# Edge rows in fewer packets, a reordered first group and a wo low part on another engine, in a graph attention layer

## The chip, the cores and the metric

The kernel runs on one core of one Trainium2 chip. The time is the device time in microseconds. A profiled execution gives a span, from its first to its last instruction, beside its own time.

## The reference

The layer normalizes 384 node vectors of 1024 numbers, applies ReLU, and runs 16-head attention over them with two projections in a row for each of query, key and value. The edges (6528 pairs of source and destination, each with a type) make an additive mask; pairs without an edge get minus infinity.

```python
h = jnp.maximum(_layernorm(x, axis=-1), 0.0)
q = h @ wq.T + bq;  k = h @ wk.T + bk;  v = h @ wv.T + bv
q2 = (q @ wiq.T + biq).reshape(N, H, D).transpose(1, 0, 2)     # N = 384, H = 16, D = 64
k2 = (k @ wik.T + bik).reshape(N, H, D).transpose(1, 0, 2)
v2 = (v @ wiv.T + biv).reshape(N, H, D).transpose(1, 0, 2)
mask = jnp.full((N, N), -jnp.inf).at[src, dst].set(w[edge_type - 1])   # the diagonal is always set
attn = softmax(einsum('hnd,hmd->hnm', q2, k2) / 8 + mask)
x + (attn @ v2, heads joined) @ wo.T + bo
```

## The kernel before

**Numbers in two parts.** Every matrix product is made of three fp32r products: high part by high part, high by low, and low by high. An operand is split by rounding it to fp32r (the high part) and subtracting that from the original (the low part). For the weights this is `split_hi` (L77, a copy on ScalarE, or L75 on VectorE) and `split_lo` (L82, a subtraction on VectorE unless another engine is given). `mm3` issues the three products (L367 high by high, L368 with the weight's low part in the projections, L369 with the activations' low part). In the output projection the roles are exchanged, and the weights stream.

**Weights in chunks.** There are 56 weight chunks of 128 x 1024 numbers, in the order v, q, iv, k, then iq and ik in turn, then eight of wo. `load(w)` (L65) brings a chunk into one of three `raw` buffers through SP's queue; a chunk's load can only start when the chunk three before it has been split. All loads named here are issued by SP, in program order.

**The order of the work.** The order is written out by hand: each engine runs its instructions in the order in which the program issues them.

**The start.** SP issues the first block of x (128 tokens, 512 KB), then the edge rows `er`, the two other blocks of x (all L96; the edge rows are L98), weight chunk 0, the edge columns `ed`, chunk 1 and two small tables. GpSimd turns the edge rows into one key per edge in `key_rows` (L182 to L184: integer to float, source times 384, plus destination), and SP writes the keys to a table `krow` in DRAM (L185), from which the row loads (L205) read them back for all partitions. Then chunk 2 is loaded. For each block t of 128 tokens, VectorE takes the statistics (L251, L254), ScalarE negates the mean (L257) and subtracts it from the first half of the columns (L280); GpSimd does the second half of blocks 0 and 1 (L282), VectorE both halves of block 2 (L284). TensorE transposes the two halves (L292), ScalarE takes the ReLU as high part (`ln_hi`, L298), and VectorE later the low part (`ln_lo`, L303). `hT` then holds the activations, tokens along the columns: 0 to 127 from block 0, 128 to 255 from block 1, 256 to 383 from block 2. On ScalarE the two `ln_hi` of block 0 stand ahead of the L257 and L280 of block 1.

GpSimd also splits weight chunk 0, in halves: high part L344, low part L346. Chunk 1 gets its high part on ScalarE (L77), after all six `ln_hi`, and its low part on GpSimd (L82), after chunk 0 and a conversion of the edge columns (L150).

**The first group.** The first output chunk (w == 0) is made of 24 products of 128 x 128 by 128 x 384, all on L414: the eight high-by-high ones first, then four at a time the ones with the low part of the weight and of the activations. The second group follows with L367, L368, L369 for each of eight k.

**The attention and the output projection.** Attention runs over 48 steps (16 heads by 3 blocks) with projection work filled in between. In step i TensorE makes the scores of step i (`do_S`, L694, one of two `s` banks), VectorE reduces those of step i - 1 (`do_ttr`, L700, which frees the bank), ScalarE takes the exponential, GpSimd normalizes (L709, after VectorE's reciprocal L708), and TensorE transposes (L714). From step 37 on, `wo_prep` splits the wo chunks 2 to 7 in the steps of `WSTEPS`. Its tuple `OPOOL` lists the chunks whose low part GpSimd makes. Chunks 4 to 6 go to a part of the buffer that held q.

```python
    def wo_prep(k):
        ...
        split(WO + k, nc.gpsimd if k in OPOOL else None, dst, k in ODVE)
        load(WO + k + 2)
```

The first half of the output projection's sums (chunks 0 to 3) is added to the residual by VectorE (`ysum`, L654) from step 43 on; chunk 4 is first used after that, in the second half.

Of the kernel before, what the change touches and what calls it, by code (L numbers as in the profile page):

```python
# [10 lines left out]
I32 = mybir.dt.int32  # L11
AF = mybir.ActivationFunctionType
OP = mybir.AluOpType

N, D, NT, KT, NP = 384, 1024, 3, 8, 8
E = 6528
EC = E // 128
# [5 lines left out]
def gnn_kernel(ctx: ExitStack, tc: tile.TileContext, x, edges, erows, etw, wq, wk, wv, wiq, wik, wiv, wo,  # L23
# [6 lines left out]
    nc = tc.nc  # L30
# [13 lines left out]
    def bank(tag):  # L44
        return psum.tile([128, 512], F32, tag=tag, name=tag, bufs={"g": 3, "a": 1}.get(tag, 2))
# [11 lines left out]
    raw, whl = {}, {}  # L57
# [33 lines left out]
    xt = [xall[:, t * D:(t + 1) * D] for t in range(NT)]  # L91
    xn = [xall[:, (NT + t) * D:(NT + t + 1) * D] for t in range(NT)]
    ert = work.tile([128, N], F32, tag="e", name="er", bufs=EB)
    er = ert[:, :2 * EC].bitcast(I32)
    for t in range(NT):
        nc.sync.dma_start(xt[t], x[t * 128:(t + 1) * 128, :])  # L96
        if t == 0:
# [28 lines left out]
    krow = dram.tile([EC, 128], F32, name="krow")  # L126
# [48 lines left out]
            nc.gpsimd.tensor_tensor(val, val, t, OP.add)  # L175

    krt = work.tile([128, N], F32, tag="e", name="kr", bufs=EB)
    kf = ert[:, :2 * EC]

    def key_rows():  # L180

        nc.gpsimd.tensor_copy(kf, er)  # L182
        nc.gpsimd.tensor_scalar(kf[:, :EC], kf[:, :EC], float(N), None, op0=OP.mult)
        nc.gpsimd.tensor_tensor(krt[:, :EC], kf[:, :EC], kf[:, EC:], OP.add)  # L184
        nc.sync.dma_start(krow.rearrange("c j -> (c j)").rearrange("(p e) -> p e", p=128), krt[:, :EC])  # L185

    rows = {}
    PA = 6
# [81 lines left out]
    def ln_row():  # L270

        ps = bank("t")
        for t in range(NT):
            nc.tensor.transpose(ps[:, t * 128:(t + 1) * 128], rstd[:, t:t + 1].to_broadcast([128, 128]), ident)
        nc.scalar.activation(rrow, ps[:, :N], AF.Copy)
# [35 lines left out]
    mask_consts()  # L311
    warm(WARM[0])
    key_rows()
    load(2)
    for s in range(NTAB):
# [55 lines left out]
    def colmm(ps, w, src, k):  # L371
        hi, lo = whl[w]
        mm3(ps[:, :N], hi[:, k * 128:(k + 1) * 128], lo[:, k * 128:(k + 1) * 128],
            src[:, 0, k, :], src[:, 1, k, :], k == 0, k == KT - 1)
# [5 lines left out]
    def evac_row(ps, hi, lo, bias):  # L380
        f = work.tile([128, N], F32, tag="e", name="f", bufs=EB)
        nc.vector.tensor_tensor(f, ps[:, :N], rrow, OP.mult)  # L382
        nc.scalar.activation(hi, f, AF.Identity, bias=bias)  # L383
        post.append(lambda: nc.vector.scalar_tensor_tensor(lo, f, bias, hi.bitcast(F32), op0=OP.add, op1=OP.subtract))
# [4 lines left out]
    def flush(last=False):  # L389
        while pend:  # L390
            pend.pop(0)()
        while last and post:
            post.pop(0)()

    def slot_head(w):
        if w > 0:
            split_hi(w + 2)
        if w != 1:
            flush()
        split_lo(w + 2)  # L400
        while post:
            post.pop(0)()
        load(w + 4)

    def proj(src, dst, bidx, extra=None):
        nonlocal w
        for m in range(8):
            slot_head(w)
            ps = bank("g")
            if w == 0:  # L410
                for a, b, ks in ((0, 0, range(KT)), (1, 0, range(4)), (0, 1, range(4)), (1, 0, range(4, KT)),
                                 (0, 1, range(4, KT))):
                    for k in ks:
                        nc.tensor.matmul(ps[:, :N], whl[0][a][:, k * 128:(k + 1) * 128], src[:, b, k, :],  # L414
                                         start=(a == b == k == 0), stop=(b == 1 and k == KT - 1))
            else:
                for k in range(KT):
                    colmm(ps, w, src, k)
                    if w == 1 and k == 3:
                        ln_row()  # L420
                        flush()
            pend.append(lambda ps=ps, m=m: evac_row(ps, dst[:, 0, m, :], dst[:, 1, m, :],
                                                bc[:, bidx * 8 + m:bidx * 8 + m + 1]))
            if extra:
                extra(m)
            w += 1
# [47 lines left out]

    vT = gtile("g2")
    proj(hT, vT, 2, extra_v)
    qT = gtile("g3")
    proj(hT, qT, 0, extra_q)

    xbd = dram.tile([N, D], F32, name="xbd")  # L480
# [50 lines left out]
    def extra_k(m):  # L531
# [5 lines left out]
        if m < 2:  # L537
            residual(m + 6)
    kT = gtile("g2")
    proj(hT, kT, 1, extra_k)  # L540
    flush(True)

# [70 lines left out]
    LT, LA = 5, 7  # L613
    PRE, RATE, RATE_O, RATE_E = 84, 7.9, 8, 8
    WSTEPS = (37, 40, 42, 44, 47, 51)
    PAR, OPOOL, ODVE = 1, (2, 3, 6), (2,)

    otile = {}
    oacc = {}
# [147 lines left out]
    for i in range(S + LA + 4):  # L767
# [14 lines left out]
        j = i - LA  # L782
# [73 lines left out]
```

## Time and profile before

| What | Value |
|---|---|
| median of 3 runs | 302.67 us (302.49 to 303.0) |
| the profiled execution's own time | 302.19 us |
| its span | 300.5 us |
| TensorE busy | 293.1 us, 1649 products |
| VectorE, ScalarE, GpSimd busy | 200.5, 154.9 and 155.7 us |
| granted TensorE clock | 0.999 |
| first product of the first group (L414) | at 12.26 us |
| first L367 of the second group | at 16.50 us |

In the profile PE is TensorE, PEld its weight loads, DVE VectorE, ACT ScalarE, POOL GpSimd, and SPq SyncE's queue, which issues transfers. A row of a timeline gives the start in us, the length in us, the engine, the line of the program, the operation, what it writes and reads, and in brackets how long the engine was idle before it and what ended that idle time. A row of the chain gives start, length and what the end of the program waited for then. A row of a table by stretches gives the stretch, its length, the busy time of PE, PEld, DVE, ACT and POOL with the instructions started in it, the granted clock, the DMA engines' share and GB/s. In the program's names of this trace, `g` stands for the large buffers and for a PSUM bank, `whl` for a split weight chunk, `lnt` for the statistics.

### The profile page before, as it was taken

The numbers are of one execution on the slowest core, as the hardware profiler recorded it, in microseconds if no ns is written. First come the engines' busy times: TensorE is split into PE (matmuls) and PEld (weight loads), VectorE is DVE, ScalarE is ACT, GpSimd is POOL, SyncE is SP. The second block draws the span as 40 slices with busy tenths as digits, with TensorE's granted clock in tenths as the row PEclk, the third lists the DMA queues.
The fourth block names the chain that finished last, engine by engine and source line by source line (L and its number), as shares of the span: only waits on it lengthen the run. The fifth ranks groups of instructions, "written<-read, shape, count | busy, mean of one in ns | idle before, by whom it ended". The sixth has DMA issues, their size and how long they took to land.

```text
span 300.5 us, 4961 instructions
## 1 busy us (share of the span) xinstructions
PE 293.1 (98%) x1649; PEld 276.1 (92%) x1649; DVE 200.5 (67%) x492; ACT 154.9 (52%) x289; POOL 155.7 (52%) x164
## 2 busy tenths in 40 slices
PE   7899999999999999999999999999999999999995
PEld 5699999999988889999999999999999998888884
DVE  2959986655956463788865576767576757696523
ACT  3874644333422213554325667777777767676310
POOL 5865766271555785730033737373746467566210
PEclk9999999999999999999999999999999999999999
DMA  7899754642686668475369997646565636910005
GB/s 233 284 297 381 281 164 171 228 143 70 217 238 224 193 217 242 142 274 198 115 169 244 217 221 173 166 127 180 155 170 139 174 81 174 381 41 0 2 0 209
DMA packets 22377, 55.12 MB, mean 183 GB/s; under 512 B 4816, under 2 KB 8400, under 8 KB 22352
## 3 DMA queue, kind: packets, MB, share of 16 engines
q1 hardware_dynamic: 19968, 52.42, 57.7%
q0 software_dynamic: 2064, 1.80, 2.0%
q10 hardware_dynamic: 320, 0.59, 0.8%
q8 instruction: 13, 0.21, 0.3%
q14 instruction: 12, 0.10, 0.1%
HBM read 40.39 MB, written 4.97 MB: 151 GB/s over the span
## 4 chain that ended last, share of the span: by engine, by line
PE 95%; DMA 2%; DVE 1%; ACT 0%; issue 0%; SPq 0%
PE g L369 21%; PE g L367 21%; PE g L368 21%; PE s L694 6%; PE a L731 6%; PE t L714 5%; PE s L369 2%; PE s L368 2%; PE s L367 2%; DMA g<-in_x_dram 2%; PE t L369 2%; PE t L367 2%; PE t L368 2%; PE g L414 1%; PE a L369 1%; PE a L367 1%
## 5 line engine op out<-in xcount | busy, mean ns | idle before, releaser
L367 PE MATMUL g<-g,whl 128*128 128x384 f32 x312 | 106.4, 341 | 0.0
L369 PE MATMUL g<-g,whl 128*128 128x384 f32 x312 | 104.5, 335 | 0.0
L368 PE MATMUL g<-g,whl 128*128 128x384 f32 x312 | 104.2, 334 | 0.0
L228 POOL DMA_INDIRECT tab<-val,idx x51 | 57.6, 1129 | 40.3 <-issue 11.3
L77 ACT ACTIVATE whl<-raw 128x1024 fp32r<-128x1024 f32 x51 | 53.4, 1051 | 31.7 <-PE g L369 20.1
L709 POOL TENSOR_TENSOR e<-e,s 128x384 f32<-128x384 f32 x48 | 39.2, 830 | 41.2 <-DVE s L708 32.9
L368 PEld LDWEIGHTS g<-g,whl 128*128 128x128 f32 x312 | 58.7, 188 | 0.0
L367 PEld LDWEIGHTS g<-g,whl 128*128 128x128 f32 x312 | 58.6, 188 | 0.0
L369 PEld LDWEIGHTS g<-g,whl 128*128 128x128 f32 x312 | 58.5, 188 | 0.0
L82 DVE TENSOR_TENSOR whl<-raw,whl 128x1024 fp32r<-128x1024 f32 x41 | 50.2, 1224 | 9.6 <-ACT whl L77 7.9
L82 POOL TENSOR_TENSOR whl<-raw,whl 128x1024 fp32r<-128x1024 f32 x11 | 26.5, 2412 | 35.6 <-ACT whl L77 31.8
L383 ACT ACTIVATE g<-f,bc 128x384 fp32r<-128x384 f32 x24 | 14.8, 618 | 53.1 <-DVE f L382 46.8
L704 ACT ACTIVATE e<-e,s 128x384 f32<-128x384 f32 x48 | 29.4, 612 | 13.0 <-DVE s L700 13.0
L724 DVE TENSOR_TENSOR pt<-t,pt 128x384 fp32r<-128x384 f32 x48 | 26.4, 550 | 13.9 <-ACT pt L723 13.3
L723 ACT ACTIVATE pt<-t 128x384 fp32r<-128x384 f32 x48 | 23.2, 484 | 13.9 <-PE t L714 13.3
L700 DVE CUSTOM_DVE_ANT_0 e<-s,ma 128x384 f32<-128x384 f32 x48 | 26.3, 550 | 2.0 <-PE s L694 1.8
L694 PE MATMUL s<-ks,qs 128*128 128x384 f32 x96 | 25.3, 344 | 0.3 <-DVE s L700 0.2
L714 PE MATMUL t<-ident,e 128*128 128x128 f32 x144 | 23.5, 271 | 0.0
L382 DVE TENSOR_TENSOR f<-g,rrow 128x384 f32<-128x384 f32 x24 | 13.3, 555 | 13.5 <-PE g L369 7.6
L714 PEld LDWEIGHTS t<-ident,e 128*128 128x128 f32 x144 | 18.8, 140 | 3.1
L378 DVE SCALAR_TENSOR_TENSOR nat<-g,bc,nat 128x384 fp32r<-128x384 f32 x16 | 9.9, 618 | 16.4 <-ACT nat L377 14.4
L731 PE MATMUL a<-pt,vhl 128*128 128x384 f32 x96 | 20.8, 351 | 0.0
(147 smaller groups left out, 414.8 us busy)
## 6 DMA issues: line engine op xcount, KB each, us to landing
ks<-nat SPq DMA_DIRECT2D x30, 192.0 KB
raw<-in_wv_dram SPq DMA_DIRECT2D x8, 512.0 KB
raw<-in_wq_dram SPq DMA_DIRECT2D x8, 512.0 KB
raw<-in_wiv_dram SPq DMA_DIRECT2D x8, 512.0 KB
raw<-in_wk_dram SPq DMA_DIRECT2D x8, 512.0 KB
raw<-in_wiq_dram SPq DMA_DIRECT2D x8, 512.0 KB
raw<-in_wik_dram SPq DMA_DIRECT2D x8, 512.0 KB
raw<-in_wo_dram SPq DMA_DIRECT2D x8, 512.0 KB
```

The costliest lines, as they stand in the source:

```text
L77: nc.scalar.activation(dst[0], raw[w], AF.Copy)
L82: (eng or nc.vector).tensor_tensor(lo, raw[w], hi.bitcast(F32), OP.subtract)
L228: nc.gpsimd.indirect_dma_start(out=tabs[c // RNG], out_offset=bass.IndirectOffsetOnAxis(ap=idx[:, c:c + 1], axis=0), in_=val[:, c:c + 1], ...
L367: nc.tensor.matmul(ps, lhi, rhi, start=first, stop=False)
L368: nc.tensor.matmul(ps, lhi, rlo, start=False, stop=False)
L369: nc.tensor.matmul(ps, llo, rhi, start=False, stop=last)
L694: nc.tensor.matmul(ps[:, :N], qs[:, o, t * 128:(t + 1) * 128], ks[:, o, s, :], start=(s == 0), stop=(s == 1))
L704: nc.scalar.activation(es[i], es[i], AF.Exp, bias=s[:, 0:1], scale=-1.0, accum_out=s[:, 1:2])
L709: nc.gpsimd.tensor_tensor(es[i], es[i], s[:, 2:3].to_broadcast([128, N]), OP.mult)
L714: nc.tensor.transpose(ps[:, k * 128:(k + 1) * 128], es[i][:, k * 128:(k + 1) * 128], ident)
L724: nc.vector.tensor_tensor(lo, pv, hi.bitcast(F32), OP.subtract)
L731: nc.tensor.matmul(ps[:, :N], vhl[:, k, p, 2 * o:2 * o + 2, :], pts[h][:, s, k, :], start=(k == 0 and s == 0), stop=(k == 2 and s == 1))
```

## The change

Three edits are made together.

1. The edge rows come as 34 rows of 2 x 192 integers (1536 bytes each) in place of 128 rows of 2 x 51 (408 bytes). `key_rows` then works on 34 partitions with 384, 192 and 192 columns, and the keys go to `krow` as 34 rows of 192. The table in DRAM holds the same keys in the same order.
2. In the first group the eight high-by-high products are made for tokens 0 to 255 first (256 columns), then for tokens 256 to 383 (128 columns). The sixteen other products stay as they are. The group has 32 products in place of 24.
3. The low part of wo chunk 4 is made by GpSimd, not by VectorE.

```diff
-    er = ert[:, :2 * EC].bitcast(I32)
+    ERP, ERC = 34, E // 34
+    er = ert[:ERP, :].bitcast(I32)
...
-    kf = ert[:, :2 * EC]
+    kf = ert[:ERP, :]
...
         nc.gpsimd.tensor_copy(kf, er)
-        nc.gpsimd.tensor_scalar(kf[:, :EC], kf[:, :EC], float(N), None, op0=OP.mult)
-        nc.gpsimd.tensor_tensor(krt[:, :EC], kf[:, :EC], kf[:, EC:], OP.add)
-        nc.sync.dma_start(krow.rearrange("c j -> (c j)").rearrange("(p e) -> p e", p=128), krt[:, :EC])
+        nc.gpsimd.tensor_scalar(kf[:, :ERC], kf[:, :ERC], float(N), None, op0=OP.mult)
+        nc.gpsimd.tensor_tensor(krt[:ERP, :ERC], kf[:, :ERC], kf[:, ERC:], OP.add)
+        nc.sync.dma_start(krow.rearrange("c j -> (c j)").rearrange("(p e) -> p e", p=ERP), krt[:ERP, :ERC])
...
-                for a, b, ks in ((0, 0, range(KT)), (1, 0, range(4)), (0, 1, range(4)), (1, 0, range(4, KT)),
-                                 (0, 1, range(4, KT))):
+                al = (0, N)
+                for a, b, ks, (n0, n1) in ((0, 0, range(KT), (0, 256)), (0, 0, range(KT), (256, N)),
+                                           (1, 0, range(4), al), (0, 1, range(4), al), (1, 0, range(4, KT), al),
+                                           (0, 1, range(4, KT), al)):
                     for k in ks:
-                        nc.tensor.matmul(ps[:, :N], whl[0][a][:, k * 128:(k + 1) * 128], src[:, b, k, :],
-                                         start=(a == b == k == 0), stop=(b == 1 and k == KT - 1))
+                        nc.tensor.matmul(ps[:, n0:n1], whl[0][a][:, k * 128:(k + 1) * 128], src[:, b, k, n0:n1],
+                                         start=(a == b == k == n0 == 0), stop=(b == 1 and k == KT - 1))
...
-    PAR, OPOOL, ODVE = 1, (2, 3, 6), (2,)
+    PAR, OPOOL, ODVE = 1, (2, 3, 4, 6), (2,)
...
-        "erows": np.ascontiguousarray(np.concatenate([np.asarray(a).reshape(128, EC) for a in (src, dst)], axis=1)),
+        "erows": np.ascontiguousarray(np.concatenate([np.asarray(a).reshape(34, E // 34) for a in (src, dst)], axis=1)),
```

## The prediction, made before the change was run

> **What bounds the kernel now.** I read the engine shares first, then the chain that ended last, then the timelines of the two places that the diff touches.
>
> ```profile
> PE 293.1 (98%) x1649; PEld 276.1 (92%) x1649; DVE 200.5 (67%) x492; ACT 154.9 (52%) x289; POOL 155.7 (52%) x164
> ```
>
> TensorE is the bound: from 12.2 to 285 us it has almost no idle time. So only two stretches can give or take time: the start, before TensorE runs dense, and the tail. The chain of waits at the start:
>
> ```profile
> 1.72 5.41 DMA g<-in_x_dram
> ...
> 7.16 1.30 DVE lnt L251 x2
> ...
> 8.96 0.73 ACT g L280
> ...
> 12.26 4.41 PE g L414 x24
> ```
>
> The second x block (x1) lands only at 7.16, three microseconds after the first, whose statistics began at 4.16. The DMA's stretches say why:
>
> ```profile
> 3.25:4.00 0.75, 0.75 (x5) 0.66 (x4) 0.00 (x0) 0.00 (x0) 0.00 (x0) 1.00 1.09 277
> 4.00:5.50 1.50, 1.50 (x9) 1.28 (x8) 1.31 (x3) 0.00 (x0) 0.96 (x3) 1.00 0.86 221
> ```
>
> The last column is GB/s: 277, then 221, against 410 from 2.50 to 3.25 and 379 from 5.50 to 7.50. The 128 edge-row packets pass in 3.25 to 4.00 (160 of its 198 packets are under 512 bytes); most of the low rate comes after them. The loss is (410-277)/410 x 0.75 + (410-221)/410 x 1.5 = 0.24 + 0.69 = 0.9 us of transfer.
>
> GpSimd at the start, then TensorE where the second weight chunk begins:
>
> ```profile
> 4.35 0.27 POOL L182 CAST er<-er 128x102 f32<-128x102 int32 x1 [1.77 <-DMA er<-in_erows_dram]
> ...
> 5.77 1.04 POOL L282 TENSOR_TENSOR g<-g,lnt 128x512 f32<-128x512 f32 x1 [0.28 <-DVE lnt L254]
> ...
> 9.81 1.36 POOL L344 CAST whl<-raw 128x512 fp32r<-128x512 f32 x2
> 11.14 2.72 POOL L346 TENSOR_TENSOR whl<-raw,whl 128x512 fp32r<-128x512 f32 x2
> ...
> 14.20 2.41 POOL L82 TENSOR_TENSOR whl<-raw,whl 128x1024 fp32r<-128x1024 f32 x1
> ```
>
> ```profile
> 16.50 0.33 PE L367 MATMUL g<-g,whl 128*128 128x384 f32 x1
> 16.68 0.33 PE L368 MATMUL g<-g,whl 128*128 128x384 f32 x1
> ```
>
> L368 is the first product with chunk 1's low part, which GpSimd ends at 14.20 + 2.41 = 16.61; it starts 0.07 us later. So the first group (L414) has no lead to give: if it ends sooner, L368 still waits for GpSimd. That low part waits in turn for ScalarE's high part (L77, 13.07 to 14.12), which stands behind the six L298 evacuations (the last at 12.20).
>
> The tail, from the chain:
>
> ```profile
> 261.43 0.24 PE g L369
> ...
> 261.70 0.04 DVE g L654
> ...
> 262.31 0.55 DVE e L700
> ```
>
> TensorE's product at 262.92 waits for L700, that for the second L654, and that L654 was released by TensorE (261.43 + 0.24), not by the low part of wo chunk 4, which VectorE ended at 260.99.
>
> [...]here 384 fp32r columns take 0.173 us start to start (20 products from 71.46 to 74.93) and 256 columns 0.117 (the tail, 293.95 to 294.18 for two)[...]; products of 128 are not shown. [...]more columns lengthen it; L184 (51 columns, 0.29 us) against L709 (384 columns, 0.83 us) agrees on the columns.
>
> **The edge rows.** [...]L182 starts 0.7 us later, at 5.05 (bounds 4.35[...] and 5.25). [...]if the low rate was theirs, x1 lands at about 7.16 - 0.9 = 6.2, and x2 and the first weight chunks as much earlier. Bounds: no gain, and 1.47 us, the idle time of L251.
>
> key_rows on GpSimd: columns go from 102/51/51 to 384/192/192. Cast: L182 0.27 and L150 (153 columns) 0.33 give 1.1 ns a column, so 0.27 + 282 x 1.1 ns = 0.58 (low end 0.5 from L344's 0.61 at 512). Multiply: 0.39 + 141 columns at 1.0 to 2.1 ns (L174, L142) = 0.53 to 0.69. Add: 0.29 to 0.83 over 333 columns is 1.6 ns, so 0.52. With 0.2 us of gaps, 1.8 (1.75 to 2.0) against 1.14 before (4.35 to 5.49).
>
> Behind it on GpSimd is L282 for block 0: it starts at 5.05 + 1.8 = 6.85, not 5.77, and ends at 7.9. TensorE's second transposes of block 0 (L292, 7.22) move to 7.95, end 0.6 later at 8.55; ScalarE's L298 goes from 7.92 to 8.6. ScalarE works in order: the small L257 follows 0.49 later (9.1), L280 0.24 after that: 9.35, not 8.96. So x1's lead is spent behind GpSimd, and 0.4 us more. L292 of block 1 follows L280 by 0.77 (10.1), L298 that by 0.70 (10.8). Before, L298 of block 2 waited for VectorE's L284 and the transposes; with x2 earlier they are ready, and four L298 run 0.49 apart: the last starts at 10.8 + 1.47 = 12.3, not 12.20. Chunk 1's high part, its low part and L368 follow: 0.1 later.
>
> Other queues: SP issues krow at 6.9, not 5.52, and raw chunk 2 behind it, which waited for x1 until 7.15 anyway. The krow write is [...]hidden in the backlog that held the row loads until 11.82; the first L217 comes at 23.6 and no row of waits names a load of rows, and uncovered it would delay VectorE's L382.
>
> **The first group.** Eight products of 384 columns become eight of 256 and eight of 128. Removed: 8 x 0.173 = 1.38. Added: 8 x 0.12 = 0.96, and 8 of 128. Bounds for one of 128: 0.06 (half of 256)[...]. I take 0.1: the f32 transposes L292 start 0.09 apart, four weight loads in 0.42. Added in sum: 0.4 us. Gained: the first eight no longer wait for L298 of block 2. With the transposes of block 2 at 11.3 they start at 11.7, end 12.65, the narrow ones, whose second half waits for the last L298 (12.9), about 13.45, and the other 16 x 0.173 = 2.77 later: 16.2. L367 may start as late as 16.6 without moving L368. So 0.4 us is free, and a narrow product costs nothing up to 0.1 + 0.4/8 = 0.15 us.
>
> **Wo chunk 4.** VectorE loses 1.23 us (259.76 to 260.99), GpSimd gains 2.40 (as its L82 rows) at 259.75 to 262.15. GpSimd is idle there for 3.50 us until 263.11, when L708 releases it: 1 us of cover; without that, L709 and the transposes behind it move by the rest. VectorE's first L654 starts 0.3 earlier, the second stays at 261.70, and L700 with it. SP's last raw load waits for this low part: 1.2 us later, needed by L77 at 278.76. Its first use, L367 at 277.09, is far off. Cost 0, bounds 0 and -0.4 (the wait at 262.5), the latter excluded by the releaser.
>
> **Sum.** +0.1 + 0 + 0: 302.19 (span 300.5 and 1.69 around it) becomes 302.3. That execution is 0.48 below the median of 302.67, so the forecast is 302.8. Of this case itself: 302.5 to 303.3 (L182 at 5.25 and 2.0 us of key_rows put L298 0.6 later).
>
> **Rivals.** (1) [...]key_rows ends by 6.1 and L282 costs nothing. Then L257 follows L298 at 8.4, L280 starts at 8.66, and blocks 1 and 2 run together: last L298 at 11.6, L368 0.6 earlier: 302.1, down to 301.2 at the ceiling of 1.47. For: 0.9 us of lost DMA rate beside these packets. Against: [...]key_rows' extra 0.7 us. (2) Slower: narrow fp32r products. It decides above 0.15 us each.[...] For: [...]no product under 256 columns in the trace.[...] (3) The low rate belongs to x1's own reads: x1 stays at 7.16, only the late rows act, and blocks 1 and 2 still follow L280 within 0.2: no change.
>
> **Chances.** 0.2% (0.6 us) is about what a measurement of this kernel can tell from no change. Likeliest case with (3): 0.36, within. Rival (1): 0.36, of which 0.32 faster (its worked price lies on the line, its ceiling far beyond) and 0.04 within. Rival (2): 0.28, slower. I give (1) as much as the likeliest case because one number, the landing of the edge rows, separates them, and before does not show it. Range 301.6 to 303.8: it takes in most of (1) and (2).
>
> **What would show it.** Right: L182 near 5.05, key_rows 1.8 us, x1's L251 before 6.5, L280 near 9.35, L414 before 12, L368 bound by L82 near 16.8, L700 after L654 unchanged at 262. Wrong: L182 before 4.5; L280 at 8.7; L414's narrow products over 0.15 us apart; L368 starting well after L82's end; any idle TensorE between 17 and 260.

## The result, and the profile after

| Kernel | Median | Lowest to highest | Runs |
|---|---|---|---|
| before | 302.66 us | 301.39 to 303.81 | 16 |
| after | 304.72 us | 303.31 to 305.67 | 16 |

The ratio after to before is 1.0064, with a 95% interval of 1.0047 to 1.0081: the change makes the kernel slower by about 2 us. The forecast was 302.8 us, no change, with a range up to 303.8; the result lies above the range. The profiled execution of after took 304.44 us, its span is 302.7 us. Lines below the start of the kernel stand one to three numbers later than before (L182 is L183, L280 is L281, L282 is L283, L292 is L293, L298 is L299, L367 to L369 are L368 to L370, L414 is L417, L694 and L700 are L697 and L703; the idle transposes of `warm`, L309 before, are L310). Idle transposes are transposes whose result nobody reads; the kernel issues them to keep TensorE busy in its gaps.

The engine shares, from the page of after:

```profile
PE 293.1 (97%) x1657; PEld 276.7 (91%) x1657; DVE 199.8 (66%) x491; ACT 154.7 (51%) x289; POOL 158.8 (52%) x165
```

TensorE is busy for the same 293.1 us, with eight products more, while the span is 2.2 us longer. So nearly the whole loss between these two executions is idle time of TensorE, and it has to be looked for by place. The chain of waits of after, first at the start:

```profile
1.25 4.25 DMA er<-in_erows_dram
...
5.56 0.51 POOL er L183
...
7.50 1.04 POOL g L283
...
8.60 0.67 PE t L293 x4
...
10.01 0.73 ACT g L281
...
12.75 4.62 PE g L417 x32
```

Before, this chain began with a block of x; now it begins with the edge rows, passes through the keys on GpSimd to block 0's subtraction, and reaches block 1 on ScalarE one microsecond later than before (10.01, not 8.96). GpSimd's timeline and TensorE's:

```profile
5.56 0.50 POOL L183 CAST er<-er 34x384 f32<-34x384 int32 x1 [2.98 <-DMA er<-in_erows_dram]
6.16 0.72 POOL L184 TENSOR_SCALAR er<-er 34x192 f32<-34x192 f32 x1
6.96 0.58 POOL L185 TENSOR_TENSOR kr<-er 34x192 f32<-34x192 f32 x1
...
14.93 2.40 POOL L82 TENSOR_TENSOR whl<-raw,whl 128x1024 fp32r<-128x1024 f32 x1 [0.68 <-ACT whl L77]
```

```profile
8.60 0.66 PE L293 MATMUL t<-ident,g 128*128 128x128 f32 x4 [1.29 <-POOL g L283]
...
12.51 4.87 PE L417 MATMUL g<-g,whl 128*128 128x256 f32 x32
17.21 0.34 PE L368 MATMUL g<-g,whl 128*128 128x384 f32 x1
17.39 0.34 PE L369 MATMUL g<-g,whl 128*128 128x384 f32 x1
```

The rows arrive 1.21 us later than before (5.56 against 4.35), the keys take 2.0 us, and TensorE idles 1.29 us for block 0's second half. The second group begins at 17.21, 0.71 later than before. L369, the first product with the low part from L82 on GpSimd (14.93 + 2.40 = 17.33), starts 0.18 us after L368, the usual distance of two such products (0.173 us where the prediction took it from before), so no wait for L82 shows. The same holds for the prediction's L368 before (16.68 after 16.50): GpSimd ends just in time there, and what a lead would gain was not seen. Whether the 0.71 us are the change's own is taken up with the experiments. The DMA's stretches of the start, last column GB/s:

```profile
3.25:4.00 0.75, 0.75 (x5) 0.65 (x4) 0.00 (x0) 0.00 (x0) 0.00 (x0) 1.00 0.90 281
4.00:5.50 1.50, 1.50 (x9) 1.27 (x8) 1.39 (x3) 0.00 (x0) 0.00 (x0) 1.00 0.83 252
```

Without the 408-byte packets (in the first stretch 10 of 67 packets are under 512 bytes, before 160 of 198) the rate is about as low as before (277 and 221 there). The lateness grows from 0.7 to 2.1 us near 160 us, where TensorE of before had no such wait. First the chain of after, then two stretches of TensorE (the third number is its busy time), of before and of after:

```profile
157.32 7.36 DMA raw<-in_wiq_dram
...
166.88 1.13 DVE whl L82
168.01 0.47 DVE e L703
168.54 0.62 PE s L697 x2
```

```profile
165.00:170.00 5.00, 5.00 (x29) 4.70 (x29) 3.40 (x13) 3.33 (x8) 3.12 (x3) 1.00 1.06 223
```

```profile
165.00:170.00 5.00, 3.39 (x20) 3.07 (x19) 3.42 (x10) 3.30 (x9) 0.89 (x2) 1.00 0.90 210
```

A weight chunk of iq, needed by ScalarE, lands 7.4 us after its issue. ScalarE's rows for that wait, of before and of after:

```profile
162.35 1.06 ACT L77 ACTIVATE whl<-raw 128x1024 fp32r<-128x1024 f32 x1 [2.26 <-DMA raw<-in_wiq_dram]
```

```profile
164.70 1.06 ACT L77 ACTIVATE whl<-raw 128x1024 fp32r<-128x1024 f32 x1 [4.97 <-DMA raw<-in_wiq_dram]
```

Behind L77 on ScalarE stands an evacuation, behind that on VectorE L379, the low part of the next chunk and the reduction L703, and that one frees the bank that TensorE waits for: it is idle for 1.6 us. The tail has the same shape as before, 2.1 us later:

```profile
263.86 0.57 issue
264.42 0.55 DVE e L703
265.03 0.62 PE s L697 x2
```

One more thing shows in the times, which give a mean granted clock for each run: of the 16 runs of after, 11 have one below 0.996; of 215 runs of the kernel before that were taken beside the experiments, 31. Within after the two kinds differ little: the eleven have a median of 304.75 us, the five others one of 304.44. So there are three things to explain: the start, the wait near 160 us, and the clock. A ratio follows the mean of the runs more than their median; where a kernel's runs lie in two groups the two differ, and the interval of the ratio is what I go by.

### The profile page after: what moved, and what is told of

The parts are those of the page before. It is cut to its first block, busy times and chain, and to the rows that moved or that the text cites. A ratio compares the mean times of both kernels' runs of the same rounds, so it can differ in the third digit from the quotient of the medians.

```text
span 302.7 us, 4977 instructions
## 1 busy us (share of the span) xinstructions
PE 293.1 (97%) x1657; PEld 276.7 (91%) x1657; DVE 199.8 (66%) x491; ACT 154.7 (51%) x289; POOL 158.8 (52%) x165
## 3 DMA queue, kind: packets, MB, share of 16 engines
HBM read 40.39 MB, written 4.97 MB: 150 GB/s over the span
## 4 chain that ended last, share of the span: by engine, by line
PE 90%; DMA 4%; DVE 1%; issue 1%; POOL 1%; ACT 1%; SPq 1%; ACTq 0%; POOLq 0%
PE g L370 20%; PE g L368 20%; PE g L369 20%; PE s L697 6%; PE a L734 6%; PE t L717 5%; DMA raw<-in_wiq_dram 2%; PE s L369 2%; PE s L370 2%; PE s L368 2%; PE g L417 2%; PE t L370 2%; PE t L369 2%; PE t L368 2%; DMA er<-in_erows_dram 1%
## 5 line engine op out<-in xcount | busy, mean ns | idle before, releaser
L368 PE MATMUL g<-g,whl 128*128 128x384 f32 x312 | 106.5, 341 | 0.0
L370 PE MATMUL g<-g,whl 128*128 128x384 f32 x312 | 104.6, 335 | 0.0
L369 PE MATMUL g<-g,whl 128*128 128x384 f32 x312 | 104.3, 334 | 0.0
L229 POOL DMA_INDIRECT tab<-val,idx x51 | 55.9, 1096 | 38.5 <-DMA tab<-val,idx 11.7
L77 ACT ACTIVATE whl<-raw 128x1024 fp32r<-128x1024 f32 x51 | 53.4, 1052 | 33.6 <-PE g L370 21.1
L82 DVE TENSOR_TENSOR whl<-raw,whl 128x1024 fp32r<-128x1024 f32 x41 | 50.2, 1223 | 13.9 <-ACT whl L77 13.9
L369 PEld LDWEIGHTS g<-g,whl 128*128 128x128 f32 x312 | 58.7, 188 | 0.0
L368 PEld LDWEIGHTS g<-g,whl 128*128 128x128 f32 x312 | 58.6, 188 | 0.0
L370 PEld LDWEIGHTS g<-g,whl 128*128 128x128 f32 x312 | 58.6, 188 | 0.0
L82 POOL TENSOR_TENSOR whl<-raw,whl 128x1024 fp32r<-128x1024 f32 x11 | 26.5, 2410 | 36.4 <-ACT whl L77 32.6
L703 DVE CUSTOM_DVE_ANT_0 e<-s,ma 128x384 f32<-128x384 f32 x48 | 26.3, 550 | 2.8 <-PE s L697 2.6
L697 PE MATMUL s<-ks,qs 128*128 128x384 f32 x96 | 25.2, 344 | 1.8 <-DVE s L703 1.8
L379 DVE SCALAR_TENSOR_TENSOR nat<-g,bc,nat 128x384 fp32r<-128x384 f32 x16 | 9.9, 617 | 18.0 <-ACT nat L378 17.0
L697 PEld LDWEIGHTS s<-ks,qs 128*128 128x128 f32 x96 | 17.2, 188 | 4.2 <-DVE s L703 3.6
```

The lines of the kernel that those rows point to most:

```text
L77: nc.scalar.activation(dst[0], raw[w], AF.Copy)
L82: (eng or nc.vector).tensor_tensor(lo, raw[w], hi.bitcast(F32), OP.subtract)
L229: nc.gpsimd.indirect_dma_start(out=tabs[c // RNG], out_offset=bass.IndirectOffsetOnAxis(ap=idx[:, c:c + 1], axis=0), in_=val[:, c:c + 1], ...
L368: nc.tensor.matmul(ps, lhi, rhi, start=first, stop=False)
L369: nc.tensor.matmul(ps, lhi, rlo, start=False, stop=False)
L370: nc.tensor.matmul(ps, llo, rhi, start=False, stop=last)
```

## The experiments

### Each edit alone

Edit 1 alone (`e1_rows34`), edit 2 alone (`e2_group`), edit 3 alone (`e3_wolow`), and edit 1 with another number of rows (`e4_rows48`). The first three edits are those of the diff. The last one is edit 1 with another number; against edit 1 one line of the kernel differs, and the array is reshaped to match:

```diff
-    ERP, ERC = 34, E // 34
+    ERP, ERC = 48, E // 48
```

> Edit 1 alone. Theory A (late rows): the edge rows land near 5.5 us[...], key_rows takes 2.0 us, the first product starts as late as with all three edits (12.5 to 12.8), the second group (L367) begins near 16.9 to 17.2, and nearly the whole +2.0 us of the three edits is here (+1.5 to +2.2). Theory B (the loss is spread over the edits): +0.4 to +0.8 us here, no wait of TensorE near 166 us. Theory C (x1's reads are slow whatever stands before them): x1's statistics begin at 7.0 to 7.4 us in this run too.

> Edit 2 alone. Theory A (late rows): L414's successor starts 0.3 us sooner than 12.26, ends within 0.2 us of before, and since L368 waits for GpSimd's low part at 16.6 the time is within 0.3 us of before. Theory B: the narrow products take their own toll, +0.3 to +0.8 us, with a later L367.

> Edit 3 alone. Theory A: no effect (within 0.3 us); L700 still follows the second L654 at 262.3 us and TensorE waits there as before. Theory B: GpSimd's 2.4 us delays L709 and the transposes behind it, +0.3 to +1.0 us.

> Edit 1 alone, but with 48 rows of 2 x 136 integers (1088 bytes)[...]. Theory A1[...]: the rows land[...] near 4.3 us, key_rows takes about 1.5 us and ends before 6.0, L282 is at most 0.2 us late, and the time is within 0.3 us of before. Theory A2 (GpSimd's wider operations are enough): still +0.5 us or more. Theory C (x1's reads are slow by themselves): x1's statistics begin at 6.9 to 7.3 us here as well; if the small packets were the cause, below 6.5.

| Kernel | Median | Ratio to before, interval | Runs | Clock below 0.996 |
|---|---|---|---|---|
| e1, 34 rows | 304.4 us | 1.0054 (1.0031 to 1.0076) | 8 | 5 |
| e2, the group | 303.09 us | 1.0020 (1.0003 to 1.0036) | 22 | 6 |
| e3, wo low part | 302.38 us | 0.9999 (0.9983 to 1.0015) | 14 | 2 |
| e4, 48 rows | 302.54 us | 0.9999 (0.9984 to 1.0013) | 22 | 4 |

For e1, Theory A held on the time (1.8 us where it said 1.5 to 2.2) and on the rows, which were usable at 5.61; its start in the profile was later than forecast (first group at 14.08, not 12.5 to 12.8), for a reason that comes below. For e2 the time is that of Theory B, for e3 Theory A held. For e4, A1 held on the time; the rows were usable at 4.55, not 4.3, the keys ended at 6.17, not before 6.0, and L283 began 0.37 us later than before's L282, not 0.2. Theory C asked when x1's statistics begin: at 8.21 in e1 and 7.63 in e4, later than any of its figures. The loss belongs to edit 1, and within it to the number 34. GpSimd's timelines, of e1 and of e4:

```profile
5.61 0.50 POOL L183 CAST er<-er 34x384 f32<-34x384 int32 x1 [3.02 <-DMA er<-in_erows_dram]
6.21 0.72 POOL L184 TENSOR_SCALAR er<-er 34x192 f32<-34x192 f32 x1
7.02 0.58 POOL L185 TENSOR_TENSOR kr<-er 34x192 f32<-34x192 f32 x1
7.56 1.03 POOL L283 TENSOR_TENSOR g<-g,lnt 128x512 f32<-128x512 f32 x1
```

```profile
4.55 0.41 POOL L183 CAST er<-er 48x272 f32<-48x272 int32 x1 [1.97 <-DMA er<-in_erows_dram]
5.05 0.58 POOL L184 TENSOR_SCALAR er<-er 48x136 f32<-48x136 f32 x1
5.71 0.46 POOL L185 TENSOR_TENSOR kr<-er 48x136 f32<-48x136 f32 x1
6.14 1.03 POOL L283 TENSOR_TENSOR g<-g,lnt 128x512 f32<-128x512 f32 x1
```

Nearly as few packets (48 of 1088 bytes) are usable 1.06 us earlier than 34 of 1536 (4.55 against 5.61). Why, no run shows. GpSimd's operations are also shorter in e4: of the 1.42 us by which its L283 starts sooner, 1.06 are the landing and 0.36 the narrower keys, so e4 does not separate the two wholly.

Edit 2 costs 0.2% with an interval that begins just above zero. Its 32 products take 4.70 us from the first to the second group, against 4.24 for the 24 before, but they also start sooner behind the evacuations. From the start of the last L298 to the second group it is 4.30 us before and 4.42 in e2, so its trace shows a tenth of a microsecond of cost, not 0.6. Edit 3 costs nothing. The three excesses add up to 0.73%, 2.2 us; the whole change has 0.64%.

### How far a late start reaches

Before, with 6, 12 or 20 idle transposes ahead of the first group (`d6_delay`, `d12_delay`, `d20_delay`).

```diff
             if w == 0:
+                for i in range(6):
+                    nc.tensor.transpose(ps[:, :128], ident, ident)
```

> The kernel before with 6 idle transposes put ahead of the first group on TensorE (about 0.56 us, TensorE stays busy). Theory P (a later start passes to the end one to one): +0.5 to +0.6 us. Theory G (the load of a projection chunk near 162 us sets the pace there, so that a small delay of the start is taken up before it): +0.0 to +0.2 us in the profiled span, and the delay of the tenth and later attention steps is less than half of that of the first group.

> The same with 12 transposes (about 1.1 us). Theory P: +1.1 us. Theory G: what goes beyond the slack of about 0.5 us passes on, +0.5 to +0.7 us. Theory R (a delay of this size makes the transfers near 157 us meet in another order, whatever caused it): +1.7 us or more, with TensorE idle over 1 us near 166 us, as in the changed kernel.

> The same with 20 transposes (about 1.9 us, the delay that the edge rows alone gave the first group in their profile). Theory P: +1.9 us. Theory G: +1.3 to +1.6 us. Theory R: over 2.2 us.

In their traces the transposes hold the group back by 0.58, 1.23 and 2.10 us (from the first of them to the group). The medians are 303.03, 303.9 and 304.38 us, the ratios 1.0021 (1.0008 to 1.0034), 1.0052 (1.0032 to 1.0071) and 1.0073 (1.0048 to 1.0097), with 22, 7 and 6 runs. Theory P, one to one, is nearest for these times. Theory R is out for d12, whose profile has no idle TensorE near 166 us; d20 lies at its limit (0.73% is 2.2 us), and its TensorE idles 0.63 us at 168.

The traces say something else, though, when all of them are laid beside before. In each, TensorE's products from 18 us to 154 us are late by one and the same amount; from 175 us on it is another. These are the two figures, with the time from the chunk's issue to its use near 160 us (us):

| Profile | Late up to 154 us | Late from 175 us on | Chunk, issue to use |
|---|---|---|---|
| after | 0.71 | 2.1 | 7.4 |
| e1 | 1.83 | 1.7 | 5.3 |
| e2 | 0.81 | 0.23 | 4.5 |
| e3 | 0.61 | 0.09 | 4.7 |
| e4 | 0.43 | 0.10 | 6.1 |
| d6 | 0.80 | 0.80 | 6.4 |
| d12 | 1.61 | 1.05 | 4.5 |
| d20 | 1.22 | 1.58 | 6.8 |

So up to about 0.55 us of a late start is given back in that stretch, unless the chunk comes late. And e3, which touches nothing at the start, begins its second group almost as late as after, because its x1 is used only at 7.78 (before: 7.16):

```profile
17.11 0.33 PE L367 MATMUL g<-g,whl 128*128 128x384 f32 x1
```

So the 0.71 us of after's start are within what single executions differ by, and in its profiled execution nearly all of the 2.1 us arises near 160 us. In e1's profile it is the other way round: 1.83 us arise at the start, and 1.7 are left.

### TensorE's rate at the start

The profile of e1 shows more than late rows. Its stretches of the start (the third column from the end is the granted clock), then TensorE's timeline:

```profile
9.00:10.50 1.50, 1.43 (x9) 0.92 (x7) 1.47 (x4) 1.12 (x3) 0.68 (x1) 0.62 1.01 330
10.50:12.00 1.50, 1.16 (x6) 1.16 (x7) 1.43 (x4) 0.29 (x2) 1.50 (x3) 0.50 0.92 345
12.00:13.50 1.50, 1.50 (x12) 1.48 (x10) 1.50 (x3) 1.25 (x3) 1.50 (x2) 0.75 0.49 185
```

```profile
8.65 0.66 PE L293 MATMUL t<-ident,g 128*128 128x128 f32 x4 [1.29 <-POOL g L283]
9.14 1.28 PE L310 MATMUL g<-ident 128*128 128x128 f32 x6
10.84 1.12 PE L293 MATMUL s<-ident,g 128*128 128x128 f32 x4 [0.41 <-ACT g L281]
11.75 1.06 PE L293 MATMUL t<-ident,g 128*128 128x128 f32 x4
```

After the idle 1.29 us the clock falls to a half, and four transposes take 1.06 to 1.12 us in place of 0.60 to 0.66. From the granted clocks of the three stretches I estimate 3.4 us at half rate in this execution ((1 - 0.62)/0.5 x 1.5 + 1.5 + 0.75). In this execution the second group starts at 18.34, against 17.21 in the one of after, which kept its clock (the first groups can't be compared so, since edit 2 lets after's start sooner). TensorE idles the same 1.29 us in both (ahead of 8.65 in e1, of 8.60 in after), so this gap alone does not decide it. That TensorE's idle time has a part in it was my guess.

To test it, I filled TensorE's gaps of after with idle transposes, 10 between the halves of block 0 and 14 in place of 6 behind it (`f_warm`):

```diff
             pss.append(ps)
+            if t == half == 0:
+                warm(10)
...
-    WARM = (20, 6, 0)
+    WARM = (20, 14, 0)
```

> The changed kernel with more idle transposes in TensorE's two gaps at the start (10 after the first half of block 0, 14 in place of 6 after the second), so that its granted clock stays up. Theory T (the lowered clock in most runs is what makes the changed kernel slow): every run has a clock of 0.997 or more, and the time is 1.0 us or more below that of the changed kernel, under 303.7. Theory U (the late edge rows alone, the clock adds little): clock 0.997 or more but still 304.2 to 305.0.

It took 303.49 us in the median of 22 runs, ratio 1.0045 (1.0030 to 1.0061), and no run has a clock below 0.996 (after: 11 of 16). In its profile every group of four transposes from 8.69 on takes 0.60 to 0.66 us. So with the idle transposes the clock stayed up in all 22, and the median is 1.2 us below after's, as Theory T said. But the runs lie in two groups: 15 from 302.91 to 303.88 and 7 from 304.79 to 305.48, and the interval of the ratio still touches that of after. Something worth 1.8 us is left that comes and goes between executions, and the lower group, too, lies above before.

### The landing near 160 us

The profiled execution of f_warm took 303.88 us, so it belongs to the lower group; the upper one was not caught in a profile. What it shows, on ScalarE, is a late chunk:

```profile
164.25 1.06 ACT L77 ACTIVATE whl<-raw 128x1024 fp32r<-128x1024 f32 x1 [4.43 <-DMA raw<-in_wiq_dram]
```

The chunk was issued at 157.05 and used at 164.25, 7.2 us later; TensorE then idles 1.06 us. In the other profiles taken so far this took from 4.5 (e2, d12) over 4.7 (before, e3) to 6.8 us (d20). To take the wait away, I had this one chunk loaded some microseconds earlier (issued at 152.8 to 155.3 in the three profiles), into a big buffer that is free at that time and that its later user, `ao`, then takes over. This was done to before, to after and to f_warm (`g_early_before`, `g_early_after`, `g_early_warm`). In the same batch, `k_keylate` is after with the keys behind block 0's subtraction on GpSimd.

```diff
-    ao = gtile("g1")
+    ao = None
...
-        if first:
+        if first and w != W0 + 2:
             load(w + 4)
+        if w == W0 + 1:
+            raw[W0 + 6] = gtile("g1").bitcast(F32).rearrange("p a k n -> p (a k n)")[:, :D]
+            nc.sync.dma_start(raw[W0 + 6], W["iq"][3])
+        if w == W0 + 4:
+            ao = gtile("g1")
```

```diff
-    key_rows()
     load(2)
-    for s in range(NTAB):
-        key_load(0, s)
...
     ln_sub(0, 512, D, nc.gpsimd)
+    key_rows()
+    for s in range(NTAB):
+        key_load(0, s)
```

> The kernel before, with one weight chunk (the fourth of iq, issued at 157.67 us and landed at 162.35) loaded into a buffer that is free there, about 152 us, so that nothing near 160 us waits for it. Theory G (that landing is a gate which takes time whenever it is late): in the kernel before it is just in time, so the gain is small: 302.2 to 302.7, at most 0.5 us. Theory N (no gate there): no change, within 0.2 us. Theory H (the loads are held back by something else, so the next one becomes the gate): slower or no gain, and a wait of L77 for a DMA stays in the trace.

> The changed kernel with the same chunk loaded early. Theory G: about 1.4 of its 2.1 us are lost where L77 waits until 164.7 for that chunk; without it the start's 0.7 us and the share of runs with a lowered clock are left: 303.3 to 303.9, and TensorE has no idle time between 165 and 170 us. Theory N: the 2.1 us stay, 304.4 to 304.9.

> The changed kernel with the chunk loaded early and with the idle transposes of f_warm that keep the clock up at the start. f_warm ran in two groups, about 303.4 and 305.2 us, both at the full clock. Theory G: the upper group is the late landing; it vanishes and all runs lie within 302.9 to 303.6, median about 303.3. Theory N: the two groups stay.

> The changed kernel with the keys (L183 to L185) issued behind the subtraction of block 0 on GpSimd in place of ahead of it; the rows still come as 34 packets. Theory A (the late rows cost only because block 0's subtraction stands behind them on GpSimd): L283 of block 0 starts at 5.8, the first group at about 11.9, L368 at 16.5 to 16.8; the time falls to 302.5 to 303.3, unless the keys now hold the subtraction of block 1. Theory B (the rows cost through the DMA or the clock, wherever the keys stand): 304 or more.

| Kernel | Median | Ratio to before, interval | Clock below 0.996 |
|---|---|---|---|
| before, chunk early | 302.29 us | 1.0003 (0.9988 to 1.0017) | 9 of 22 |
| after, chunk early | 304.24 us | 1.0039 (1.0025 to 1.0053) | 13 of 22 |
| after, gaps filled | 303.49 us | 1.0045 (1.0030 to 1.0061) | 0 of 22 |
| after, both | 302.61 us | 1.0009 (0.9996 to 1.0022) | 0 of 22 |
| after, keys later | 303.41 us | 1.0025 (1.0009 to 1.0042) | 7 of 22 |

With both, the loss of 0.64% against plain before is down to 0.09%, whose interval holds zero, and lies apart from those of after, of the gaps alone and of the early chunk alone. Each alone takes off about 0.2%, its interval touching that of after. Theory G holds for g_early_warm in that the group near 305 is gone; its median of 302.61 lies below the 302.9 to 303.6 forecast. Before itself gains nothing that can be told from zero, which is Theory N as much as G. For g_early_after Theory G's 303.3 to 303.9 was too low: 13 of its 22 runs have the lowered clock, and the nine others, with a median of 304.07, are not fast either. In its profile the clock stands at 0.50 from 9 to 15 us and the first group starts only at 14.62. In g_early_warm six runs still lie between 303.70 and 304.47; what sets those apart I did not find. ScalarE's row of the early chunk in g_early_warm, which follows the work before it without a wait, and TensorE's stretch:

```profile
159.66 1.05 ACT L77 ACTIVATE whl<-g 128x1024 fp32r<-128x1024 f32 x1
```

```profile
165.00:170.00 5.00, 5.00 (x31) 5.00 (x30) 3.17 (x11) 3.44 (x8) 2.76 (x3) 1.00 0.89 238
```

TensorE has no idle time there. Its start is as late as that of after (ScalarE's evacuations before 150 us stand 0.75 us behind those of before), yet from 175 us on only 0.17 us of that is left. In g_early_before the start happened to be 0.62 late and 0.04 is left at the end. So here, too, 0.55 to 0.6 us of a late start are swallowed between 155 and 175 us. Where the chunk took 6.8 us or more (after, d20, and f_warm with 0.82 before and 1.6 behind), time was added there instead.

k_keylate answers for the order on GpSimd. L283 of block 0 starts at 5.68 and TensorE's second transposes follow the first without a gap, as Theory A said. The time falls from 1.0064 to 1.0025, intervals apart: a large part of what the late rows cost is what stands behind them on GpSimd. The write of the keys, which comes later still in this kernel (the keys end at 8.66, not 7.54), is thereby not what costs. The median of 303.41 ends 0.1 us above Theory A's range. Its profiled execution had a slow start for another reason, which TensorE's timeline shows:

```profile
6.64 1.11 PE L293 MATMUL s<-ident,g 128*128 128x128 f32 x4 [0.69 <-ACT g L281]
7.55 1.06 PE L293 MATMUL t<-ident,g 128*128 128x128 f32 x4
8.40 1.49 PE L310 MATMUL g<-ident 128*128 128x128 f32 x6
```

These are durations as in e1 (1.06 to 1.11 us for four, not 0.60 to 0.66) from the first transposes on, with no gap of 1.3 us ahead of them, while the granted clock of the page reads 1.00 throughout. Before's own trace opens at a low rate too, also with a recorded clock of 1.00:

```profile
1.43 4.53 PE L309 MATMUL g<-ident 128*128 128x128 f32 x20 [1.43 <-POOL ident masks.py:199]
```

That is 0.23 us for one transpose, against 0.15 for the six at 7.66 (0.88 us). In before the rate has risen by 6.73 (0.65 us for four transposes); in k_keylate it is still low at 13.28 (0.99 us). So a start can be slow in two ways, by a fall after a gap, as in e1, or by a rise that comes late, and the recorded clock doesn't show the second. The operation's own duration is the surer sign, and the counts of runs with a lowered clock, zeros included, may miss some. Slow starts occur without the change as well (31 of 215); with it a lowered clock is more frequent (11 of 16).

### The kernel before, without both

If slow starts and late landings are in before as well, taking them out of before should beat both kernels. `h_before_warm` has more idle transposes in before's own gaps, `h_before_warm_early` also the early chunk.

```diff
-    WARM = (20, 6, 0)
+    WARM = (24, 14, 0)
```

> The kernel before with more idle transposes in its own gaps at the start: 24 in place of 20 ahead of block 0, 14 in place of 6 behind it (about 0.145 us each, so 0.6 and 1.2 us more in gaps of 0.8 and 1.2 us). Theory T (the start runs slowly in the executions in which TensorE has idled too long, also without the change): no run has a clock below 0.996, the group near 304 us is gone, median 302.2 to 302.5. Theory U (the slow starts are nothing that TensorE's idle time sets): a sixth of the runs or more stays near 304, and the median does not fall.

> The same with the fourth chunk of iq loaded early (as in g_early_before). g_early_before had 13 runs at the full clock with a median of 302.2 and 9 at 303.5. Theory T with G: all runs lie in the lower group: 302.0 to 302.3, faster than the kernel before and than the changed kernel. Theory U: two groups stay, median 302.3 or more.

Of 44 runs none has a clock below 0.996; of the 43 of before beside them, 12. Those 12 have a median of 303.88, the other 31 one of 302.56: in before, too, the runs with a lowered clock are 1.3 us longer. Theory T is right on the clock. The times gain little: 302.7 us, ratio 0.9991 (0.9972 to 1.0010), where it said 302.2 to 302.5, and 302.43 us, ratio 0.9987 (0.9972 to 1.0001), where it said 302.0 to 302.3 and a single group; four of those runs lie at 303.5 and above. The second is well below after; against before its gain of about 0.4 us is not proven.

These runs allow a fairer account of the change, with both kernels treated alike. The last column is the quotient of the two ratios; its intervals are my estimate, with the two measured ones taken as independent.

| Treatment of both kernels | Changed kernel | Kernel before | What the change then costs |
|---|---|---|---|
| none | 1.0064 | 1 | 1.0064 (1.0047 to 1.0081) |
| gaps filled | 1.0045 | 0.9991 | 1.0054 (1.0030 to 1.0079) |
| chunk early | 1.0039 | 1.0003 | 1.0036 (1.0016 to 1.0056) |
| both | 1.0009 | 0.9987 | 1.0022 (1.0003 to 1.0041) |

Both together take away about two thirds of the loss. Neither alone takes away an amount that is clear of the noise, and at face value keeping the clock up takes away least. About 0.2%, 0.7 us, is left that neither explains.

## Why the prediction was wrong

**The step that failed: "only two stretches can give or take time", the start and the tail.** TensorE is the bound, and a start's delay does pass from 17 to 154 us unchanged. But "almost no idle time" in one execution of before is not the same as no wait: at 162.35 ScalarE had waited 2.26 us for a chunk whose landing lay just early enough. The forecast put this stretch at nothing, and it put the start's cost at a shift in time and nothing else. I listed idle TensorE between 17 and 260 us as a sign of being wrong, and it came, 1.61 us from 166.93 to 168.54. The start itself was forecast 0.1 us late, and 0.71 showed, of which single executions of kernels with an untouched start show as much (e3: 0.61). So the sum failed by what it left out: with the chunk early and the gaps filled in both kernels, 0.64% becomes 0.22%.

**The edge rows: direction right, size short.** L182 started at 5.56, not 5.05, beyond my bound of 5.25. The term that failed is the landing: the 0.7 us in the forecast were my estimate, and why 34 rows are this late was not shown. What showed was 1.2 us more than with 128 rows, not 0.7; 48 rows were usable 0.2 us later, which is within the spread of the 128-row profiles (4.33 to 4.68). The keys took 2.0 us, the upper end of 1.75 to 2.0.

**x1's lead: wrong.** The 0.9 us of lost rate were put on the 408-byte packets. Without them the rate from 3.25 to 5.50 is 281 and 252 GB/s, and x1 is used at 7.34, not 6.2. Over all profiles it is used between 6.81 and 8.42 with 34 rows (six of them) and between 6.54 and 7.90 with 128 (nine), so no lead shows. Rival (3) was right on that: the rate is low whatever the edge rows look like. But (3) ended at no change, because it left the late rows' cost at 0.2 us. This lead was meant to pay for the late rows in the forecast; in fact L280's block 1 came at 10.01 (forecast 9.35), the last L298 at 12.93 (12.3), L368 at 17.39 (16.78). Against this one execution of before the start's sum should have been 0.7 us, not 0.1.

**The first group: right.** A narrow product takes (4.70 - 8 x 0.117 - 16 x 0.173)/8 = 0.124 us, within my bounds and below the 0.15 from which I let it cost. Rival (2), a narrow product above 0.15 us, is wrong; that it said "slower", as it came out, is luck. (My 0.1 for it rested on transposes that start 0.09 us apart; in before's trace they start 0.11 apart and more.) I took 0.4 us for the group's growth and 0.46 was measured. The lead that was to hide it came as well: in after the group starts 0.36 us behind the start of block 2's last transposes (12.51 after 12.15; forecast 0.4), before it was 0.75 us. From the start of the last evacuation to the second group it is 4.30 us before (12.20 to 16.50) and 4.28 after (12.93 to 17.21). Alone, edit 2 costs 0.2%, hardly more than can be measured.

**Wo chunk 4: right.** Cost 0, alone 0.9999. The reduction at 264.42 still follows the second ysum of VectorE, and GpSimd is idle for 0.90 us behind the low part, close to the 1 us of cover that was forecast.

**What was in no step.** First, that TensorE idles more at the start was counted as time, not as a reason for a lower rate (with its gaps filled none of 22 runs has a lowered clock, without 11 of 16). The forecast put its second transposes 0.7 us later and never asked what the clock does; the second group starts at 18.34 in e1, with the lowered clock, and at 17.21 in after. Second, the landing near 160 us. Treated in both kernels, the two together account for about two thirds of the loss (1.0064 down to 1.0022); the share of each is not settled.

**What stays open.** Where the remaining 0.2% goes, and what marks the upper group of f_warm. Then, why the chunk's landing is so uneven. It is issued just behind the transfers into a `ks` buffer (L567 before), which come from two queues; in three profiles where it landed latest (after, f_warm, d20) ScalarE's queue had issued its two in 1.45 us, and where it landed within 5.3 us in 2.05 us or more; e4 and d6, with 2.72 and 2.26 us, lie between (6.1 and 6.4 us), so this is not all of it. Whether that order is the cause, I did not try. So it stays open, too, whether the change makes the late landing likelier or after's profiled execution merely caught it. The start's lateness alone does not bring it about: e2 was later there than after, and its chunk took 4.5 us.

## What to carry to other kernels

A transfer of few, wide rows can land later than one of many narrow ones (34 rows were usable at 5.56 us in after, 128 at 4.35 in before, 48 at 4.55 in e4): try more than one row count, and look at who stands behind its first reader in the order of its engine (L283 started at 7.50 behind the keys in after, at 5.68 ahead of them in k_keylate). At the start of a kernel, a gap on TensorE can be more than a gap (in e1, 1.29 us of idle time and then transposes at 1.06 to 1.12 us for four, not 0.60 to 0.66): look at the durations of the same operation right after it, in more than one execution. A wait that ends just in time in one profile is no cover (L77 had waited 2.26 us in before, 4.97 in after); before calling a shift of some tenths free, look down the whole program for transfers on which an engine already waits. And before taking a shift between two profiles for the change's, look at it in a kernel that doesn't touch the place.

## What was unexpected of the hardware

- 34 rows of 1536 bytes were usable at 5.56 to 5.64 us in five profiles (after, e1, f_warm, g_early_after, g_early_warm), 48 rows of 1088 bytes at 4.55 in one, 128 rows of 408 bytes at 4.33 to 4.68 in nine.
- Four f32 transposes take 0.60 to 0.66 us or 1.06 to 1.12 us at the start, in some executions of the same kernel and not in others, and the recorded clock can read 1.00 beside the longer ones (k_keylate).
- An fp32r product of 128 columns takes 0.124 us (worked out above), one of 256 columns 0.117: here the narrower one is not cheaper.
- The same load of x1 is used between 6.54 (d20) and 7.90 us (e2) in kernels that don't touch the edge rows; a single profile's landing is uncertain by half a microsecond and more.
- The same 512 KB chunk needed between 4.4 (h_before_warm) and 7.4 us (after) from issue to use in the stretch at 157 us.
